# Layer 3 of a four-layer graph attention kernel: denominators from the exponentials' own sums, and head sums on half-width column tiles

## The chip, the cores and the metric

The kernel runs on one NeuronCore of a Trainium2 chip. TensorE multiplies matrices into PSUM, which has eight banks of 128 rows by 512 f32 values. VectorE and ScalarE compute on SBUF and PSUM. GpSimd does small steps on SBUF. SyncE issues the transfers. Each engine takes its instructions in the order in which the program lists them, and semaphores tie the engines to each other. The metric is the device time of one execution in microseconds. The profiled execution took 3,227.98 us; the three timed runs took 3,219.42, 3,227.3 and 3,229.8 us.

## The reference

There are 128 graphs of 128 nodes with 512 features, and four attention layers, one after the other; each normalizes the features, takes their positive part, attends over the neighbours, and adds the result to the features. The change is in the last layer, which has H = 8 heads of k = 64 features:

```python
def _L3_gnn_ref(x, A, W_proj, W_att, b_att):
    xp = jnp.einsum('bnd,do->bno', x, W_proj)
    xh = xp.reshape(B, N, H, k).transpose(0, 2, 1, 3)
    a_src = jnp.einsum('bhnk,hk->bhn', xh, W_att[:, :k])
    a_dst = jnp.einsum('bhnk,hk->bhn', xh, W_att[:, k:])
    scores = a_src[:, :, :, None] + a_dst[:, :, None, :] + b_att[None, :, None, None]
    scores = jax.nn.leaky_relu(scores, negative_slope=NEG_SLOPE)
    scores = jnp.where((A > 0)[:, None, :, :], scores, NEG_INF)
    att = jax.nn.softmax(scores, axis=-1)
    out = jax.nn.relu(jnp.einsum('bhij,bhjk->bhik', att, xh))
    return out.transpose(0, 2, 1, 3).reshape(B, N, H * k)

h = jnp.maximum(_layernorm(x, axis=-1), 0.0)
x = x + _L3_gnn_ref(h, adj, L3_gnn_W_proj, L3_gnn_W_att, L3_gnn_b_att)
```

The softmax is a division of two sums. For each node i and head, the numerator is the sum over j of exp(score) times the features of j, and the denominator is the sum over j of exp(score).

## The kernel before

One graph is one stream of steps: `graph` (line 1053) runs `layer0` to `layer3` for it, and the nodes lie on the 128 partitions. Up to 13 graphs (`FLYING`) are in flight at once. A planner written in the kernel (`Scheduler`, line 158) merges their streams into one order for each engine. It keeps a model of time: `Step.estimate` (line 70) gives each step a duration by engine, operation and size, and `issue` (line 288) takes, among the steps that could start first, the one of the graph that is most behind its due times. This order is fixed when the program is built. All steps are issued from one line, so every instruction of the profile has line 310, and groups are told apart by the names of their tiles.

Buffers come from pools with a fixed number of copies. The ones that matter here are `bank` (eight PSUM banks), `x3` (three buffers for layer 3's features, called `fx` in the code), `e3` (three for its attention matrices, eight heads of 128 x 128), `f3` (four small ones) and `t` (five). `give_back` returns a buffer when the last reader has been listed.

`layer3` (line 909) goes like this for a graph. The normalized features are transposed and projected; the 528 columns of the product are, for each head, two attention terms and 64 features. Two copies on ScalarE bring them into `fx`, where each head has 67 columns: two terms, 64 features, and a last one that GpSimd sets to one (line 917). The scores of all heads are built by VectorE with the mask and the row maxima. ScalarE then makes eight passes with Prelu and eight with Exp over the heads, each with a bias of its own for every row. The exponentials are turned round: they go through DRAM in blocks (`exchanged`, on SyncE's queue) and are transposed in squares by VectorE; the last five graphs (`late`) use TensorE's transpose instead.

The sums follow in two halves of four heads. For each half there is one bank and a group of four matmuls: stationary are the 128 x 128 turned exponentials of a head, moving are its 64 features and the column of ones. So the 65th column of each result is the denominator. VectorE inverts the four denominators out of the bank and multiplies the 4 x 64 sums with them into `t`. At the end one VectorE step adds the positive part to the node features `xt`, which SyncE writes out.

In the profile `fx` is named x, the exponentials are e (or ht for the late graphs, which are turned into that buffer), the small tile with terms, maxima and reciprocals is f. Layers 0 to 2 take their denominators in another way, in `attention` (line 683): Exp has an `accum_out`, which leaves the sum of the row beside the result. In the profile such an exponential is followed by an instruction of its own on ScalarE, ACTIVATION_READ_ACCUMULATOR. An f32 matmul appears as two pairs of LDWEIGHTS (PEld) and MATMUL (PE).

Of the kernel before, what the change touches and what calls it, by code (L numbers as in the profile page):

```python
# [11 lines left out]
AF = mybir.ActivationFunctionType  # L12
ALU = mybir.AluOpType
# [6 lines left out]
SLOPE = 0.2  # L20
# [22 lines left out]
def size(ap):  # L43
    n = 1
    for count in ap.shape[1:]:
        n *= count
    return n


class Step:  # L50
# [19 lines left out]
    def estimate(self, name, outs, ins, kw):  # L70

        if name == "dma_start":
            moved = size(outs[0]) * outs[0].shape[0] * 4
            if self.engine == "POOL":
                self.moves = moved / 165e3
                return 1.0, 3
            run = 4 * min(a.shape[-1] for a in outs + ins)
            self.moves = moved / (280e3 if run > 512 else 220e3 if run > 128 else 130e3)
            busy = 0.5 if max(len(a.shape) for a in outs + ins) > 2 else 0.35
            return busy, (2.2 if moved > 16384 else 1.3)  # L80
        n = max(size(a) for a in outs[:1] + ins)
        if self.engine == "PE":
            if name == "transpose":
                return 0.109, 0.2
            return 2 * max(0.00084 * size(outs[0]), 0.108), 0.2
        if self.engine == "DVE":
            if name == "bn_stats":
                return 0.6, 0.12
            if name == "bn_aggr":
                return 0.09, 0.12  # L90
            per = 1 / 960
            if name == "tensor_scalar" and n >= 256:
                per /= 2
            return n * per + 0.07, 0.12
        if self.engine == "ACT":
            pointers = sum(isinstance(kw.get(k), bass.AP) for k in ("bias", "scale"))
            busy = n * 0.00081 + 0.105 + (0, 0.075, 0.135)[pointers]
            return busy + 0.1 * ("accum_out" in kw), 0.15
        if self.engine == "POOL":
            if kw.get("op") == ALU.pow or ALU.pow in kw.get("ops", ()):  # L100
                return 0.6, 0.1
            return (0.25 if n <= 16 else 0.55 if name == "tensor_scalar" else 1.3), 0.1
        raise ValueError(name)
# [54 lines left out]
class Scheduler:  # L158
# [14 lines left out]
    def give_back(self, *aps):  # L173
        for ap in aps:
            name = ap.tensor.name
            tag = self.tag_of.pop(name)
            heapq.heappush(self.returned[tag], self.last_use.get(name, 0.0))
# [157 lines left out]
def kernel(  # L335
# [24 lines left out]
    B, P, D = x.shape  # L360
# [4 lines left out]
    H3 = l3_watt.shape[0]  # L365
    K3 = l3_watt.shape[1] // 2
# [12 lines left out]
    T = Engine("PE", nc.tensor)  # L379
    V = Engine("DVE", nc.vector)  # L380
    A = Engine("ACT", nc.scalar)
    G = Engine("POOL", nc.gpsimd)
    S = Engine("SP", nc.sync)
    sched = Scheduler()
    give_back = sched.give_back

    def bank():
        return Take(ps, [P, 512], "bank", 8)

    def tile_of(tag, bufs, *shape):  # L390
        return Take(work, [P, *shape], tag, bufs)
# [15 lines left out]
    E1, E2, E3 = 2 * H1, 2, 2  # L407
# [180 lines left out]
    def blocks_of(t):  # L588

        return [t[:, i : i + P] for i in range(0, t.shape[1], P)]  # L590

    def transposed(blocks, tag, bufs):

        n = len(blocks)
        r = yield tile_of(tag, bufs, n * P)
        pt = yield bank()
        yield Group(
            [T.transpose(pt[:, j * P : (j + 1) * P], b, ident) for j, b in enumerate(blocks)]
        )
        yield A.copy(r, pt[:, : n * P])  # L600
        give_back(pt)
        return blocks_of(r)
# [63 lines left out]
    def repeated(cols):  # L666
        n = cols.shape[1]
        return cols.unsqueeze(1).to_broadcast([P, Q // n, n])
# [240 lines left out]
    def layer3(xt, mask, late):  # L909

        h = yield from norm_relu(xt)
        ht = yield from transposed(blocks_of(h), "ht", 3)
        give_back(h)
        yield Until("wp")

        fx = yield tile_of("x3", 3, H3, E3 + K3 + 1)
        yield G.memset(fx[:, :, E3 + K3 :], 1.0)
        half = H3 // 2
        yield from projected(
            ht,  # L920
            KC,
            [w.rearrange("p h k -> p (h k)") for w in wpx],
            2,
            [fx[:, g : g + half, : E3 + K3] for g in (0, half)],
        )
        give_back(ht[0])
        f = yield tile_of("f3", 4, 4, H3)
        f, mx, rz = f[:, :2], f[:, 2], f[:, 3]
        yield G.tensor_tensor(f, fx[:, :, :E3].rearrange("p h s -> p s h"), b_l3, ALU.add)

        e = yield tile_of("e3", 3, H3 * P)
        if late:
            heads = e.rearrange("p (h c b) -> p h c b", h=H3, b=Q)
        else:
            heads = e.rearrange("p (c h b) -> p h c b", h=H3, b=Q)
            rows = yield from rows_in_dram(repeated(f[:, 0]), H3)
            yield S.dma_start(out=e.rearrange("p (c f) -> p c f", c=R), in_=rows)
        mask3 = mask.rearrange("p (c b) -> p c b", b=Q)

        for g in range(0, H3, 4):  # L940
            part = [heads[:, g + j] for j in range(4)]
            if late:
                pt = yield from spread(f[:, 0, g : g + 4])
                part = pt.rearrange("p (h c b) -> p h c b", h=4, b=Q)
                part = [part[:, j] for j in range(4)]
            yield Group(
                [
                    V.tensor_tensor_reduce(
                        out=heads[:, g + j],
                        in0=part[j],  # L950
                        in1=mask3,
                        scale=1.0,
                        scalar=LOWEST,
                        op0=ALU.add,
                        op1=ALU.max,
                        accum_out=mx[:, g + j : g + j + 1],
                    )
                    for j in range(4)
                ]
            )  # L960
            if late:
                give_back(pt)
        give_back(mask)
        yield G.tensor_tensor(mx, mx, f[:, 1], ALU.add)
        yield A.activation(out=mx, in_=mx, func=AF.Prelu, alpha=SLOPE)
        yield G.tensor_scalar(mx, mx, -1.0, None, ALU.mult)
        for bias, func in ((f[:, 1], dict(func=AF.Prelu, alpha=SLOPE)), (mx, dict(func=AF.Exp))):
            for k in range(H3):
                yield A.activation(
                    out=heads[:, k], in_=heads[:, k], bias=bias[:, k : k + 1], **func  # L970
                )
        et = []
        if late:
            for g in range(0, H3, 4):
                et += yield from transposed(blocks_of(e)[g : g + 4], "ht", 3)
        else:
            to = yield from exchanged(e, "et3", 2)

            yield V.transpose(
                e.rearrange("p (h r b) -> p r h b", h=H3, b=Q),  # L980
                to.rearrange("p (r h b) -> p r h b", h=H3, b=Q),
            )
            give_back(to)
            et = blocks_of(e)
        t = yield tile_of("t", 5, D)
        for i in range(2):
            pa = yield bank()
            p3 = pa[:, : half * (K3 + 1)].rearrange("p (h k) -> p h k", h=half)
            yield Group(
                [  # L990
                    T.matmul(
                        p3[:, k - i * half, :],
                        lhsT=et[k],
                        rhs=fx[:, k, E3:],
                        start=True,
                        stop=True,
                    )
                    for k in range(i * half, (i + 1) * half)
                ]
            )  # L1000
            r = rz[:, i * half : (i + 1) * half]
            yield V.reciprocal(r, p3[:, :, K3])
            yield V.tensor_tensor(
                t[:, i * half * K3 : (i + 1) * half * K3].rearrange("p (h k) -> p h k", k=K3),
                p3[:, :, :K3],
                r.unsqueeze(2).to_broadcast([P, half, K3]),
                ALU.mult,
            )
            give_back(pa)
        give_back(e, fx, f)  # L1010
        if late:
            give_back(et[0], et[4])
        yield V.scalar_tensor_tensor(xt, t, 0.0, xt, ALU.max, ALU.add)
        give_back(t)
# [133 lines left out]
```

## Time and profile before

| what | value |
|---|---|
| profiled execution | 3,227.98 us |
| its span, first to last instruction | 3,226.2 us |
| median of the timed runs | 3,227.3 us |
| TensorE multiplications, busy | 3,189.4 us, 15,386 instructions |
| TensorE weight loads, busy | 2,497.0 us |
| VectorE busy | 2,857.0 us |
| ScalarE busy | 2,468.5 us |
| GpSimd busy | 855.9 us |
| mean granted TensorE clock | 0.994 of full speed |
| layer 3's sums: multiplications (x,e and x,ht) | 2,048 of 65 columns |
| ScalarE's accumulator reads, layers 0 to 2 | 896, mean 187 ns |

Busy time of TensorE's multiplications is the union of their records. A record lasts longer than the distance to the next one, since multiplications overlap in the array; the distance between starts tells what one costs in a row of them. LDWEIGHTS have a row of their own because they run beside multiplications.

### The profile page before, as it was taken

How to read it: one execution, taken by the hardware profiler on the slowest of the kernel's cores; microseconds unless marked ns; L12 is line 12 of the kernel's file. 1: busy time of each engine (PE TensorE's matmuls, PEld its weight loads, DVE VectorE, ACT ScalarE, POOL GpSimd, SP SyncE). 2: the span in 40 equal slices, each digit the busy share in tenths (PEclk: the TensorE clock that was granted, in tenths of full speed). 3: DMA queues.
4: the chain of work that ended last, by engine and by line, in shares of the span. 5: the costliest groups of instructions: out<-in, count | busy, mean ns of one | idle time of the engine just before them, and what ended most of it. 6: DMA issues, size and time to landing. Idle time of an engine off the chain costs nothing.

```text
span 3226.2 us, 60294 instructions
## 1 busy us (share of the span) xinstructions
PE 3189.4 (99%) x15386; PEld 2497.0 (77%) x15386; DVE 2857.0 (89%) x11663; ACT 2468.5 (77%) x7224; POOL 855.9 (27%) x2313
## 2 busy tenths in 40 slices
PE   8999999999999999999999999999999999999998
PEld 6777777777777777777777777777777777777786
DVE  6888888999998989999998999998999989989876
ACT  5677777778777877777877777777777777778867
POOL 1232222222222222222222222222222222222222
PEclk8999999999999999999999999999999999999999
DMA  6245555556556656655555555555555655555432
GB/s 173 52 114 137 144 143 152 153 150 154 150 144 157 153 141 155 155 144 155 155 146 141 157 153 151 153 152 141 151 151 151 154 150 149 143 159 149 110 101 66
DMA packets 770082, 460.39 MB, mean 143 GB/s; under 512 B 344776, under 2 KB 702408, under 8 KB 769736
## 3 DMA queue, kind: packets, MB, share of 16 engines
q1 hardware_dynamic: 765560, 456.53, 54.6%
q8 instruction: 123, 2.02, 0.3%
q14 instruction: 223, 1.83, 0.2%
q10 hardware_dynamic: 4176, 0.02, 0.1%
HBM read 299.00 MB, written 157.33 MB: 141 GB/s over the span
## 4 chain that ended last, share of the span: by engine, by line
PE 91%; DVE 3%; DMA 3%; ACT 1%; issue 1%; POOL 0%; SPq 0%; ACTq 0%; DVEq 0%; POOLq 0%
PE bank L310 91%; DVE e L310 1%; DMA e<-d 1%; DMA d<-r 1%; DMA row<-d 1%; DMA et<-exchanged 0%; DVE st L310 0%; POOL st L310 0%; SPq L310 0%; DVE products L310 0%; DVE xt L310 0%; ACT e L310 0%; DVE t L310 0%; DVE y L310 0%; ACT ht L310 0%
## 5 line engine op out<-in xcount | busy, mean ns | idle before, releaser
L310 PE MATMUL bank<-w2x,y 128*128 128x257 f32 x4096 | 968.6, 381 | 1.7 <-DVE y L310 1.7
L310 PE MATMUL bank<-w1x,ht 128*128 128x344 f32 x3072 | 953.9, 454 | 2.6 <-ACT ht L310 2.6
L310 PEld LDWEIGHTS bank<-w2x,y 128*128 128x128 f32 x4096 | 763.9, 190 | 157.3 <-issue 32.8
L310 PEld LDWEIGHTS bank<-w1x,ht 128*128 128x128 f32 x3072 | 570.3, 191 | 257.2 <-issue 9.3
L310 ACT ACTIVATE e<-e,f 128x128 f32<-128x128 f32 x2176 | 707.2, 390 | 3.1 <-DVE c L310 3.1
L310 POOL TENSOR_SCALAR st<-st 128x1 f32<-128x1 f32 x1024 | 311.1, 308 | 1185.8 <-DVE st L310 993.9
L310 ACT ACTIVATE e<-e,c 128x128 f32<-128x128 f32 x1408 | 533.1, 394 | 116.9 <-DVE c L310 60.2
L310 PE MATMUL bank<-wpx,ht 128*128 128x264 f32 x2048 | 497.1, 386 | 0.3 <-ACT ht L310 0.3
L310 ACT ACTIVATE h<-xt,st 128x512 f32<-128x512 f32 x512 | 411.3, 810 | 83.9 <-POOL st L310 74.4
L310 PEld LDWEIGHTS bank<-wpx,ht 128*128 128x128 f32 x2048 | 387.8, 190 | 97.9 <-issue 22.2
L310 DVE CUSTOM_DVE_ANT_0 e<-e,m 128x128 f32<-128x128 f32 x1484 | 337.8, 286 | 23.5 <-DMA e<-d 23.3
L310 DVE BATCH_NORM_STATS2 st<-xt 128x6 f32<-128x512 f32 x512 | 340.8, 679 | 0.5 <-DMA xt<-in_x_dram 0.5
L310 POOL TENSOR_TENSOR st<-st,minus_half 128x1 f32<-128x1 f32 x512 | 297.0, 599 | 23.6 <-POOL st L310 0.2
L310 PEld LDWEIGHTS bank<-x,e 128*128 128x128 f32 x1968 | 254.8, 191 | 62.2 <-issue 29.8
L310 PEld LDWEIGHTS bank<-et,xl 128*128 128x128 f32 x2048 | 264.7, 192 | 36.5 <-issue 8.8
L310 PE MATMUL bank<-et,xl 128*128 128x128 f32 x2048 | 270.1, 275 | 0.4 <-ACT et L310 0.4
L310 PE MATMUL bank<-h,et 128*128 128x512 f32 x512 | 263.8, 598 | 3.3 <-ACT et L310 1.9
L310 PE MATMUL bank<-x,e 128*128 128x65 f32 x1968 | 246.8, 268 | 8.5 <-DVE e L310 2.1
L310 ACT COPY xl<-bank 128x344 f32<-128x344 f32 x384 | 167.7, 437 | 108.1 <-PE bank L310 103.9
L310 ACT COPY ht<-bank 128x512 f32<-128x512 f32 x274 | 159.6, 582 | 114.9 <-PE bank L310 113.7
L310 ACT ACTIVATE t<-t 128x512 f32<-128x512 f32 x256 | 160.3, 627 | 88.1 <-DVE t L310 87.3
L310 DVE TENSOR_TENSOR y<-bank,b 128x512 f32<-128x512 f32 x256 | 175.1, 684 | 36.0 <-PE bank L310 34.7
(85 smaller groups left out, 4342.4 us busy)
## 6 DMA issues: line engine op xcount, KB each, us to landing
e<-d SPq DMA_DIRECT2D x123, 512.0 KB
exchanged<-e SPq DMA_DIRECT2D x492, 128.0 KB
et<-exchanged SPq DMA_DIRECT2D x123, 512.0 KB
xt<-in_x_dram SPq DMA_DIRECT2D x128, 256.0 KB
out_dram<-xt SPq DMA_DIRECT2D x128, 256.0 KB
e<-d SPq DMA_DIRECT2D x125, 256.0 KB
exchanged<-e SPq DMA_DIRECT2D x480, 64.0 KB
et<-exchanged SPq DMA_DIRECT2D x120, 256.0 KB
```

Source lines behind the costliest of these rows:

```text
L310: method(*args, **kw)
```

## The change

Four things change, all for layer 3 and in the planner's model of it:

- The features `fx` lose the column of ones and the memset that sets it: 66 columns for each head.
- The exponentials get `accum_out=rz[:, k]`, so that ScalarE leaves the denominators in `rz`. One reciprocal of all eight follows the last exponential on VectorE.
- The sums of all heads go into one bank, 8 x 64 = 512 columns. Each head's matmul is split into two by the output rows: one with columns 0 to 63 of the turned exponentials as stationary operand, one with columns 64 to 127. The first writes rows 0 to 63 of the bank, the second rows 64 to 127. In the built program these have a tile size of 128 x 64 and the tile positions (0, 0) and (0, 64). All sixteen are one group, so nothing comes between them on TensorE.
- VectorE multiplies the whole bank with the eight reciprocals in one step.

The planner is told 0.07 us for a matmul with fewer than 128 output rows; before, it was told 0.216 us for a matmul of up to 128 columns.

```diff
@@ Step.estimate @@
             if name == "transpose":
                 return 0.109, 0.2
+            if outs[0].shape[0] < 128:
+                return 0.07, 0.2
             return 2 * max(0.00084 * size(outs[0]), 0.108), 0.2
@@ layer3 @@
-        fx = yield tile_of("x3", 3, H3, E3 + K3 + 1)
-        yield G.memset(fx[:, :, E3 + K3 :], 1.0)
+        fx = yield tile_of("x3", 3, H3, E3 + K3)
...
-            [fx[:, g : g + half, : E3 + K3] for g in (0, half)],
+            [fx[:, g : g + half] for g in (0, half)],
...
-        for bias, func in ((f[:, 1], dict(func=AF.Prelu, alpha=SLOPE)), (mx, dict(func=AF.Exp))):
-            for k in range(H3):
-                yield A.activation(
-                    out=heads[:, k], in_=heads[:, k], bias=bias[:, k : k + 1], **func
-                )
+        for k in range(H3):
+            yield A.activation(
+                out=heads[:, k],
+                in_=heads[:, k],
+                func=AF.Prelu,
+                bias=f[:, 1, k : k + 1],
+                alpha=SLOPE,
+            )
+        for k in range(H3):
+            yield A.activation(
+                out=heads[:, k],
+                in_=heads[:, k],
+                func=AF.Exp,
+                bias=mx[:, k : k + 1],
+                accum_out=rz[:, k : k + 1],
+            )
+        yield V.reciprocal(rz, rz)
...
-        for i in range(2):
-            pa = yield bank()
-            p3 = pa[:, : half * (K3 + 1)].rearrange("p (h k) -> p h k", h=half)
-            yield Group(
-                [
-                    T.matmul(
-                        p3[:, k - i * half, :],
-                        lhsT=et[k],
-                        rhs=fx[:, k, E3:],
-                        start=True,
-                        stop=True,
-                    )
-                    for k in range(i * half, (i + 1) * half)
-                ]
-            )
-            r = rz[:, i * half : (i + 1) * half]
-            yield V.reciprocal(r, p3[:, :, K3])
-            yield V.tensor_tensor(
-                t[:, i * half * K3 : (i + 1) * half * K3].rearrange("p (h k) -> p h k", k=K3),
-                p3[:, :, :K3],
-                r.unsqueeze(2).to_broadcast([P, half, K3]),
-                ALU.mult,
-            )
-            give_back(pa)
+        pa = yield bank()
+        p3 = pa.rearrange("p (h k) -> p h k", h=H3)
+        yield Group(
+            [
+                T.matmul(
+                    p3[lo : lo + P // 2, k, :],
+                    lhsT=et[k][:, lo : lo + P // 2],
+                    rhs=fx[:, k, E3:],
+                    start=True,
+                    stop=True,
+                )
+                for k in range(H3)
+                for lo in (0, P // 2)
+            ]
+        )
+        yield V.tensor_tensor(
+            t.rearrange("p (h k) -> p h k", h=H3),
+            p3,
+            rz.unsqueeze(2).to_broadcast([P, H3, K3]),
+            ALU.mult,
+        )
+        give_back(pa)
```

## The prediction

> **What bounds the kernel.** I began with the page: busy time per engine, and the slices of the span.
>
> ```profile
> span 3226.2 us, 60294 instructions
> PE 3189.4 (99%) x15386; PEld 2497.0 (77%) x15386; DVE 2857.0 (89%) x11663; ACT 2468.5 (77%) x7224; POOL 855.9 (27%) x2313
> ...
> PE   8999999999999999999999999999999999999998
> ```
>
> TensorE's multiply queue is busy for 99% of the span, in every slice but the first and the last. Busy shares overstate a pipelined engine, so the chain of waits comes next; its columns are start, length, engine and count.
>
> ```profile
> 525.63 2633.99 PE bank L310 x12782
> ```
>
> From 525.63 us on, 2,634 us of the chain are TensorE work in its own order, with no wait in between. Before it and behind it the chain hops over other engines, but the multiplier's idle time in all is only 31.6 us (the sum of its waits). How much room do the others have? The busy time by stretch says:
>
> ```profile
> core 0: us, PE busy (x) PEld busy (x) DVE busy (x) ACT busy (x) POOL busy (x), PEclk, DMA share, GB/s
> ...
> 1000.00:2000.00 1000.00, 1000.00 (x4837) 785.56 (x4836) 910.04 (x3742) 784.52 (x2297) 272.85 (x738) 1.00 0.58 151
> ```
>
> In this stretch TensorE never stops, VectorE has 9% free, ScalarE 22%. So time on TensorE's path counts in full, and the others' time only once one of them runs out of room. What a pass of the layer-3 sums costs is read from TensorE's timeline (start, length, name, count); spacing of starts, not length, is the price, since passes overlap.
>
> ```profile
> 1601.64 1.00 PE L310 MATMUL bank<-x,e 128*128 128x65 f32 x8
> 1602.48 1.95 PE L310 MATMUL bank<-w2x,y 128*128 128x257 f32 x8
> 1604.27 2.48 PE L310 MATMUL bank<-w1x,ht 128*128 128x344 f32 x8
> ...
> 1607.86 1.02 PE L310 MATMUL bank<-h,et 128*128 128x512 f32 x2
> 1608.72 1.05 PE L310 MATMUL bank<-et,xl 128*128 128x128 f32 x8
> 1609.61 2.48 PE L310 MATMUL bank<-w1x,ht 128*128 128x344 f32 x8
> ```
>
> An f32 matmul is two passes, each a weight load and a multiplication. Eight passes with 65 moving columns take 1602.48 - 1601.64 = 0.84 us, or 0.105 each. Eight with 128 columns (et,xl) take 1609.61 - 1608.72 = 0.89 us, 0.111 each. Half the columns are no cheaper, so something else than the columns sets both: the load of 128 stationary columns. The pure price of a moving column comes from the 512-column passes: (1608.72 - 1607.86) / 2 / 512 = 0.84 ns. A 65-column pass would need 0.055 us if its load were free; the load makes it 0.105.
>
> **The change, part by part.** The other prices are in the groups by form (busy us, mean ns, idle before).
>
> ```profile
> L310 PE MATMUL bank<-w2x,y 128*128 128x257 f32 x4096 | 968.6, 381 | 1.7 <-DVE y L310 1.7
> ...
> L310 PEld LDWEIGHTS bank<-x,e 128*128 128x128 f32 x1968 | 254.8, 191 | 62.2 <-issue 29.8 <-POOL f L310 4.0 <-POOL st L310 3.3
> ...
> L310 ACT ACTIVATION_READ_ACCUMULATOR e<-e,c 128x1 f32 x896 | 168.0, 187 | 0.0
> ...
> L310 DVE TENSOR_TENSOR t<-bank,f 128x256 f32<-128x256 f32 x256 | 105.1, 411 | 5.7
> ...
> L310 DVE RECIPROCAL f<-bank 128x4 f32<-128x4 f32 x256 | 44.2, 173 | 33.4 <-PE bank L310 30.7
> ...
> L310 DVE RECIPROCAL c<-c 128x4 f32<-128x4 f32 x128 | 21.2, 165 | 2.2 <-ACT e L310 1.2
> ...
> L310 DVE TENSOR_TENSOR y<-bank,b 128x512 f32<-128x512 f32 x256 | 175.1, 684 | 36.0 <-PE bank L310 34.7
> ...
> L310 POOL MEMSET x<- 128x8 f32 x128 | 14.4, 113 | 186.6 <-PE bank L310 186.6
> ```
>
> *TensorE, what goes.* Each graph has 8 heads x 2 passes x 0.105 = 1.68 us of such sums; 128 graphs make 215 us.
>
> *TensorE, what comes.* Each head becomes two matmuls, one for each half of the output rows: 8 x 2 x 2 = 32 passes, each loading 64 columns and streaming 64. Streaming 64 columns costs 64 x 0.84 = 0.054 us. Loading 64 costs 0.105 / 2 = 0.053 us if a load's price goes by its columns. No record of before uses half of the array, so the pass is bounded: 0.027 us if the two halves load and stream side by side (two passes in 0.054), 0.054 if they take turns, 0.105 if a half load costs as much as a whole one. The 32 passes are then 0.86, 1.73 or 3.36 us. I take 0.86: the nearest rows show loads running beside multiplications already (weight loads 2,497 us and multiplications 3,189 us in a span of 3,226 us), the two halves write different rows, and neighbours in the order always use different halves.
>
> *Going into the halves and out again.* No row shows what it costs. The lower bound is nothing: in the timeline above, passes of different shapes follow each other at their usual spacing. The upper bound is an array that empties at each end: a 257-column pass lasts 0.381 us but is spaced 0.224 (1604.27 - 1602.48 over 8), a tail of 0.16, and the next load, 0.19, is no longer hidden; 0.35 an end, 0.70 a graph. I take the tail alone at both ends, 0.32, since loads ran beside multiplications in every row.
>
> So a graph's sums take 0.86 + 0.32 = 1.18 us in place of 1.68: 0.50 us, times 128 = 64 us off the path. (The planner's new 0.07 us for a half orders the steps; no price is taken from it.)
>
> The Trainium skill bears on both choices, once each way. "TensorEngine Tiling (Array Packing)", Key Properties, says that tiles load and multiply independently, and that a change of tiling mode drains the engine; with the drain at my upper price the saving is 1.68 - 0.86 - 0.70 = 0.12 us a graph, 15 us in all. "TensorE: Matmul & The Clock Gate", Part 3, says that a load overlaps a running multiplication only where its row group differs; the halves of this change share all 128 rows, so by it load and stream would add up, 16 x 0.107 + 0.32 = 2.03 us, 45 us slower. The overlapping loads of before use all rows too, so the trace already contradicts that page for whole-width loads; no run so far shows it for halves.
>
> *ScalarE.* The 1,024 exponentials of layer 3 get a running sum, which adds a read of the accumulator: 1,024 x 0.187 = 191 us, and 4 ns on each exponential (394 against 390). In the 1,000 us stretch 41 graphs pass, so ScalarE goes from 785 to 785 + 41 x 8 x 0.191 = 847 us of about 980, 86%. Hidden behind TensorE; without that cover it would be 1.5 us a graph.
>
> *VectorE.* Two reciprocals (0.173) and two products of 256 columns (0.411) become one reciprocal of 8 (0.165, the row of 4) and one product of 512 out of a bank (0.684, the y<-bank,b row): 1.168 - 0.849 = 0.32 us less, 41 us in all. It goes to 897 of 980 us, 92%. Worth nothing on the path.
>
> *GpSimd.* 128 memsets of 0.113 us go, with their 186.6 us of waiting for the features' buffer at the head of that queue, in front of the norms' small steps. The copy that fills the buffer, on ScalarE, takes over the wait; it stood behind the memset already, so it starts no later. Off the path: nothing.
>
> *New waits.* The reciprocal now waits for the eighth exponential instead of for a bank; behind it stand VectorE's steps of other graphs, the product comes much later. On SyncE the exchange of the exponentials starts 8 x 0.191 = 1.5 us later, with other graphs' transfers queued behind. The planner allows 0.1 us for a read that takes 0.187, so both queues may stand 8 x 0.087 = 0.7 us longer than planned. Cover: thirteen graphs in flight and a TensorE queue with no gap. If the cover went, 0.7 x 128 = 90 us. No DMA is added. One bank is held instead of two in turn.
>
> *The tail.* In the last graph ScalarE's chain is bare: +1.5 us, less 0.3 on VectorE: +1 us.
>
> Sum: the profiled execution took 3,228.0 us (span 3,226.2), close to the median of 3,227.3. 3,228 - 64 + 1 = **3,165 us**. Its bounds: 1.68 - 0.86 = 0.82 us a graph gives 3,123; 0.12 gives 3,213.
>
> **The rivals.**
> *The halves take turns* (slower). One multiplication or one load at a time, whatever half it is for: 1.73 + 0.32 = 2.05 us a graph, +0.37 x 128 = +47, 3,275 us; with an array that empties fully 3,324, with free switches 3,234. It decides as soon as a pass costs (1.68 - 0.32) / 32 = 0.0425 us or more. For it: TensorE is one queue in order, and no row of before shows two multiplications side by side. Against it: the halves share no output row, and loads do run beside multiplications.
> *A half load costs a whole one* (far slower): 3.36 + 0.32 is 2.0 us more a graph, about 3,484 us. For it: the 65-column pass shows a cost that ignores the moving width. Against it: nothing direct.
> *The gain is lost to lateness.* The denominators are late by 0.7 us a graph, VectorE at 92% cannot catch up, and TensorE gets gaps: between half and all of the 64 us goes, 3,195 to 3,228 us. For it: VectorE already waits 76 us for exponentials in other layers' reciprocals. Against it: it has 9% free, and TensorE waited 31.6 us in all.
>
> **How the numbers follow.** Forecast 0.58, turns 0.27, lateness 0.10, whole loads 0.05. The likeliest time is 3,165 us, its own range 3,123 to 3,213. About 0.3% (10 us, the spread of the three runs) can be told from no change. Faster: 0.58 + half of lateness = 0.63; same: the other half and a sliver of turns, 0.07; slower 0.30. For 8 in 10 the range reaches from 3,125 into the cheaper part of turns, 3,290.
>
> **What would show it.** Right: starts in the layer-3 run average 0.03 us, the run with what precedes and follows takes near 1.2 us, and TensorE still has no gap. Wrong: starts 0.05 us or more apart (turns), near 0.1 (whole loads), a long first pass or a late next one (the switch), or gaps on TensorE that end on the exponentials or the reciprocals (lateness).

## The result, and the profile after

The changed kernel is slower. Its median is 3,266.5 us against 3,228.6 us for the kernel before on the same chip, a ratio of 1.0127 with a 95% interval of 1.0104 to 1.0150. That is 38 us more, where 63 us less had been forecast. The profiled execution took 3,266.5 us.

The page of the changed kernel: span, busy time, and the chain of waits by engine.

```profile
span 3264.6 us, 64927 instructions
PE 3155.1 (97%) x17434; PEld 2394.0 (73%) x17434; DVE 2839.4 (87%) x11407; ACT 2542.8 (78%) x8248; POOL 894.9 (27%) x2185
...
PE 43%; DMA 24%; DVE 19%; ACT 8%; issue 3%; SPq 2%; POOL 2%; DVEq 0%; ACTq 0%; POOLq 0%
```

The same chain before:

```profile
PE 91%; DVE 3%; DMA 3%; ACT 1%; issue 1%; POOL 0%; SPq 0%; ACTq 0%; DVEq 0%; POOLq 0%
```

TensorE's busy time fell by 34 us, while the span grew by 38; the rest of the span, in which TensorE stands, grew from 37 to 110 us. The chain, which was 91% TensorE before, is now 43% TensorE; transfers, VectorE and ScalarE have the rest. This share shows that TensorE now waits for others, but it does not measure the loss: of the kernels below, e3 is the fastest with 60%, and e4 is 4.9% slower than the kernel before with 75%.

The stretch from 1,000 to 2,000 us, with the columns named:

```profile
core 0: us, PE busy (x) PEld busy (x) DVE busy (x) ACT busy (x) POOL busy (x), PEclk, DMA share, GB/s
...
1000.00:2000.00 1000.00, 972.43 (x5396) 738.09 (x5395) 889.51 (x3594) 793.69 (x2588) 285.10 (x686) 1.00 0.57 148
```

TensorE, which had no gap here before, stands for 27.6 us of 1,000. VectorE (890) and ScalarE (794) have as much room as before. So no engine is full, and yet the work goes slower: in the traces, layer 3 of one graph follows that of another after 24.40 us before and 24.75 us now (the mean over graphs 30 to 110).

TensorE's waits in the changed kernel (waited for, us in total, times, longest):

```profile
PE bank L312 <- DMA et<-dealt: 39.8, 27, 3.3
PE bank L312 <- ACT ht L312: 31.4, 34, 2.6
PE bank L312 <- ACT h L312: 5.8, 6, 1.4
```

They end on dealt exponentials of layers 0 and 2 and on copies of turned features (ht). These steps have nothing to do with layer 3's sums. Now the sums themselves, on TensorE's timeline (start, length, name, count; the last line is the queue of weight loads):

```profile
1608.44 2.48 PE L312 MATMUL bank<-w1x,ht 128*128 128x344 f32 x8
1610.75 1.02 PE L312 MATMUL bank<-x,et 128*128 128x512 f32 x2
1611.62 0.60 PE L312 MATMUL bank<-ident,h 128*128 128x128 f32 x4
...
1615.52 2.48 PE L312 MATMUL bank<-w1x,ht 128*128 128x344 f32 x8
1617.92 1.15 PE L312 MATMUL bank<-x,e 128*64 128x64 f32 x32
1619.01 1.12 PE L312 MATMUL bank<-h,et 128*128 128x512 f32 x2
1619.97 0.60 PE L312 MATMUL bank<-ident,h 128*128 128x128 f32 x4
...
1617.92 1.01 PEld L312 LDWEIGHTS bank<-x,e 128*64 128x64 f32 x32 [0.48 <-issue]
```

A run of 32 half-width passes takes 1619.01 - 1617.92 = 1.09 us. Getting in costs the w1x group ahead of it 1617.92 - 1615.52 = 2.40 us instead of 1610.75 - 1608.44 = 2.31; getting out makes the two h,et passes last 1619.97 - 1619.01 = 0.96 instead of 0.87. In all 1.28 us; the median over 115 such runs is 1.279 (0.093 in, 1.082, 0.104 out). Two whole groups took 2 x 0.847 = 1.69 us before, by the same measure: 0.41 us a graph more.

That comparison is not quite fair to the halves, because what stands behind a group differs between the two orders. A whole group of before costs 0.85 us ahead of the short ident,h group, where most of them stand, but 0.89 ahead of w2x,y. Experiment e9 below has whole matmuls at exactly the places where the changed kernel has halves. The same place in it:

```profile
1629.88 2.48 PE L312 MATMUL bank<-w1x,ht 128*128 128x344 f32 x8
1632.20 1.89 PE L312 MATMUL bank<-x,e 128*128 128x64 f32 x16
1633.93 1.08 PE L312 MATMUL bank<-h,et 128*128 128x512 f32 x2
1634.84 0.60 PE L312 MATMUL bank<-ident,h 128*128 128x128 f32 x4
```

Here the run takes 1633.93 - 1632.20 = 1.73 us, getting in costs nothing, and the two h,et passes behind it last 0.91. By the same measure the median over 117 runs is 1.79 us (0.00 in, 1.73, 0.06 out). So in the changed kernel's own order the halves save 0.51 us a graph, 65 us in all. The part of the change that the forecast rested on did what was expected, and still the kernel lost.

The other new prices, from the groups by form (busy us, mean ns, idle before):

```profile
L312 ACT ACTIVATION_READ_ACCUMULATOR e<-e,f 128x1 f32 x1024 | 193.3, 189 | 0.0
...
L312 DVE TENSOR_TENSOR t<-bank,f 128x512 f32<-128x512 f32 x128 | 86.7, 677 | 22.4 <-PE bank L312 22.3
...
L312 DVE RECIPROCAL f<-f 128x8 f32<-128x8 f32 x128 | 24.7, 193 | 8.2 <-ACT e L312 8.2
```

VectorE stands for only 8.2 us, in all 128 graphs together, before it can invert the eight denominators. The exponentials' sums are not what is late.

### The profile page after: what moved, and what is told of

It reads as the page before. It is cut to its first block, busy times and chain, and to the rows that moved or that the text cites. A ratio compares the mean times of both kernels' runs of the same rounds, so it can differ in the third digit from the quotient of the medians.

```text
span 3264.6 us, 64927 instructions
## 1 busy us (share of the span) xinstructions
PE 3155.1 (97%) x17434; PEld 2394.0 (73%) x17434; DVE 2839.4 (87%) x11407; ACT 2542.8 (78%) x8248; POOL 894.9 (27%) x2185
## 2 busy tenths in 40 slices
DMA packets 770103, 460.69 MB, mean 141 GB/s; under 512 B 344776, under 2 KB 702408, under 8 KB 769736
## 4 chain that ended last, share of the span: by engine, by line
PE 43%; DMA 24%; DVE 19%; ACT 8%; issue 3%; SPq 2%; POOL 2%; DVEq 0%; ACTq 0%; POOLq 0%
PE bank L312 43%; DMA d<-r 8%; DVE e L312 6%; DMA row<-d 5%; ACT e L312 5%; DMA e<-d 5%; DMA et<-dealt 5%; DVE st L312 2%; DVE xt L312 2%; DVE products L312 2%; SPq L312 2%; DVE t L312 2%; DVE y L312 1%; POOL st L312 1%; DVE c L312 1%
## 5 line engine op out<-in xcount | busy, mean ns | idle before, releaser
L312 PE MATMUL bank<-w2x,y 128*128 128x257 f32 x4096 | 956.1, 382 | 5.0 <-DVE y L312 4.9
L312 ACT ACTIVATE e<-e,f 128x128 f32<-128x128 f32 x2176 | 772.7, 391 | 3.9 <-DVE c L312 3.9
L312 ACT ACTIVATE e<-e,c 128x128 f32<-128x128 f32 x1408 | 539.7, 395 | 157.1 <-DVE c L312 81.4
L312 POOL TENSOR_SCALAR st<-st 128x1 f32<-128x1 f32 x1024 | 331.6, 329 | 1096.6 <-DVE st L312 907.6
L312 DVE BATCH_NORM_STATS2 st<-xt 128x6 f32<-128x512 f32 x512 | 347.4, 679 | 1.2 <-DMA xt<-in_x_dram 1.2
L312 POOL TENSOR_TENSOR st<-st,minus_half 128x1 f32<-128x1 f32 x512 | 307.9, 607 | 28.0
L312 PE MATMUL bank<-h,et 128*128 128x512 f32 x512 | 270.9, 612 | 39.7 <-DMA et<-dealt 36.6
L312 DVE CUSTOM_DVE_ANT_1 e<-row,m 128x128 f32<-128x128 f32 x361 | 138.9, 390 | 97.3 <-DMA row<-d 97.0
L312 DVE SCALAR_TENSOR_TENSOR xt<-bank,c,xt 128x512 f32<-128x512 f32 x256 | 185.5, 733 | 35.9 <-PE bank L312 35.8
L312 PEld LDWEIGHTS bank<-ident,h 128*128 128x128 f32 x1024 | 126.8, 141 | 113.0 <-issue 69.0
```

The costliest lines, as they stand in the source:

```text
L312: method(*args, **kw)
```

## The experiments

The ratios are to the kernel before on the same chip, with 95% intervals. "Order" is the order in which each engine's queue lists its instructions.

| kernel | order planned with | ratio | interval |
|---|---|---|---|
| changed kernel | half matmul at 0.070 us | 1.0127 | 1.0104 to 1.0150 |
| e1 sums alone | whole, 0.216 | 1.0054 | 1.0039 to 1.0069 |
| e2 tiles alone | half, 0.070 | 1.0290 | 1.0273 to 1.0308 |
| e3 changed | half, 0.108 | 0.9949 | 0.9935 to 0.9964 |
| e4 changed | half, 0.070; transfers 1.5 us slower | 1.0487 | 1.0471 to 1.0502 |
| e5 changed | half, 0.080 | 1.0173 | 1.0149 to 1.0197 |
| e6 changed | half, 0.125 | 1.0135 | 1.0120 to 1.0150 |
| e7 before | whole, 0.140 | 1.0352 | 1.0331 to 1.0373 |
| e8 changed, 14 graphs | half, 0.070 | 1.0100 | 1.0081 to 1.0119 |
| e9 whole matmuls | exactly the changed kernel's | 1.0238 | 1.0220 to 1.0256 |
| e10 whole matmuls | exactly e3's | 1.0084 | 1.0069 to 1.0099 |
| e11 before with halves | exactly that of before | 0.9963 | 0.9950 to 0.9976 |
| e12 before | whole, 0.220 | 1.0551 | 1.0536 to 1.0567 |
| e13 cheap turned load | exactly the changed kernel's | 1.0147 | 1.0132 to 1.0162 |
| e14 cheap turned load | exactly e12's | 1.0532 | 1.0514 to 1.0549 |
| e15 cheap turned load | exactly that of before | 1.0003 | 0.9994 to 1.0012 |
| e16 changed | half, 0.106 | 1.0115 | 1.0099 to 1.0132 |
| e17 one product later | the changed kernel's but for TensorE | 1.0185 | 1.0167 to 1.0204 |
| e18 one product later | e12's but for TensorE | 1.0657 | 1.0636 to 1.0678 |

### The parts by themselves: e1 and e2

e1 takes the denominators from the exponentials and keeps whole matmuls of 64 columns in two banks.

```diff
-        fx = yield tile_of("x3", 3, H3, E3 + K3 + 1)
-        yield G.memset(fx[:, :, E3 + K3 :], 1.0)
+        fx = yield tile_of("x3", 3, H3, E3 + K3)
...
+                bias=mx[:, k : k + 1],
+                accum_out=rz[:, k : k + 1],
...
+        yield V.reciprocal(rz, rz)
...
-            yield V.reciprocal(r, p3[:, :, K3])
```

> The kernel before, with the denominators taken from the exponentials' own sums and without the column of ones; the matmuls stay whole (128 output rows, now 64 columns), in two groups and two banks. Theory (TensorE's saving was real, and TensorE lost its lead over the other engines, so that it now stands waiting for late transfers and copies): TensorE is as loaded as before, so nothing shows; 3,215 to 3,240 us, TensorE without gaps from 1,000 to 3,000 us. Rival (the running sums make ScalarE, the reciprocal and the exchange late): slower, 3,250 us or more, with gaps on TensorE.

It took 3,241.4 us, just above what the theory allowed, and TensorE was busy for 999 of 1,000 us. Up to graph 120 it is level with the kernel before (the sums of that graph start at 3,157 us in both traces); the loss, 13 us between the two spans, lies in the last graphs. There few graphs are left to cover ScalarE's longer chain, but the order differs there too, and the two were not told apart.

e2 keeps the column of ones and both banks, and splits the matmuls.

```diff
-                        p3[:, k - i * half, :],
-                        lhsT=et[k],
+                        p3[lo : lo + P // 2, k - i * half, :],
+                        lhsT=et[k][:, lo : lo + P // 2],
...
+                    for lo in (0, P // 2)
```

> The kernel before, with its column of ones, its two banks and its two reciprocals out of the banks; only the matmuls are split into half-width tiles of 65 columns, and the planner is told 0.07 us for each. Theory (lost lead): gaps on TensorE as in the changed kernel, 3,230 to 3,290 us. Rival (running sums are what is late): the saving shows, 3,150 to 3,185 us, with no gaps.

It took 3,316.0 us, slower than either theory allowed. Getting in and out is paid twice here. Compared at like places, a group of 16 half passes takes 0.77 us ahead of ident,h and 0.81 ahead of w2x,y, where a whole group of before took 0.85 and 0.89. So the halves save 0.08 us a group, 0.16 a graph, 20 us in all. That explains why it gained little, not why it lost 3%. TensorE has gaps (969 busy of 1,000 us) as in the changed kernel.

### The planner's price: e3 to e8

Five kernels change what the planner believes, and e8 changes the number of graphs in flight, with the buffers that are sized by it; no instruction of the work changes. The first edit is that of e3; e5 has 0.08 and e6 has 0.125 in its place. The second is e4's, the third e8's, all in the changed kernel. The last is e7's, in the kernel before.

```diff
-                return 0.07, 0.2
+                return 0.108, 0.2
...
-            return busy, (2.2 if moved > 16384 else 1.3)
+            return busy, (3.7 if moved > 16384 else 2.8)
...
-FLYING = 13
+FLYING = 14
...
+            if size(outs[0]) == 65:
+                return 0.14, 0.2
```

> The changed kernel, with the planner told 0.108 us for a half matmul, so that a graph's sums cost 1.73 us in its model, as before. The instructions are the same, only their order is that of a planner that believes TensorE to be as loaded as before. Theory (the order planned with cheap tiles asks for more than the other queues deliver): part of the loss goes, 3,190 to 3,245 us. Rival (running sums): nothing changes, 3,255 to 3,275 us.

> The changed kernel, with the planner told 1.5 us more for the landing of every transfer (3.7 and 2.8 us in place of 2.2 and 1.3). The chain of waits of the changed kernel has dealt exponentials that land after 5.5 to 7 us once in every four graphs. Theory in the form that the planner's too short transfers let TensorE run into them: the gaps behind et<-dealt get smaller, 3,160 to 3,240 us. Rival (running sums): 3,255 us or more. If neither, the order decides for reasons that neither theory names.

> The changed kernel with the planner told 0.080 us for a half matmul: the changed kernel's trace shows 1.28 us for a run of 16 (0.093 to get in, 1.082 from the first start to the next group's, 0.104 to get out), and 1.28 / 16 = 0.080. Theory that the price told was too low: a good part of the way from 3,266 to 3,209 us, 3,200 to 3,240. Rival (which order comes out is chance, and only the loss of TensorE's lead makes chance count): anything from 3,190 to 3,290, with no regard to the price.

> The changed kernel with the planner told 0.125 us for a half matmul (2.00 us a graph, more than before). Theory (an order planned with a dearer TensorE gives the other queues room): as with 0.108 or better, 3,180 to 3,215 us. Rival (chance): anywhere from 3,190 to 3,290.

> The kernel before, instruction by instruction, but with its 65-column matmuls told as 0.14 us each, 1.12 us a graph, which is what the changed kernel tells for its own. Theory (a cheap-TensorE order is harmless as long as TensorE itself is the one slow engine, since the real matmuls then hold everything up and the others catch up): 3,220 to 3,245 us, TensorE without gaps. Rival (this kind of order is bad by itself, with or without tiles): 3,255 us or more, with gaps on TensorE.

> The changed kernel with 14 graphs in flight instead of 13 and everything else the same. Theory (TensorE runs into late results because too little finished work lies ahead of it): more graphs put more work ahead, 3,190 to 3,245 us. Rival (the number in flight does not matter, the order of the queues does): within 3,250 to 3,290, or no better than chance.

e3 gave 3,209.0 us, faster than the kernel before; the same instructions in the changed kernel's order are 1.8% slower. It looked as if a dearer TensorE in the plan were the remedy, and e5 and e6 contradict that: the price that the trace shows (0.080) gives 1.0173, a still dearer one (0.125) gives 1.0135. Telling the planner of slower transfers gave the worst of these, 1.0487. A fourteenth graph in flight changed little. The theory of a lost lead then fell with e7. That is the kernel before without a single half-width matmul, in an order planned with a cheap TensorE; its matmuls are as dear as ever, so by the theory TensorE had to stay the one slow engine. The same stretch of its trace (columns as above):

```profile
1000.00:2000.00 1000.00, 969.65 (x4626) 754.68 (x4625) 875.26 (x3579) 752.66 (x2199) 258.80 (x705) 0.99 0.58 144
```

TensorE stands for 30 us of 1,000 in it, and the kernel loses 3.5%. What e3 has in the same stretch:

```profile
1000.00:2000.00 1000.00, 990.75 (x5529) 757.49 (x5528) 911.42 (x3683) 816.58 (x2647) 270.35 (x704) 1.00 0.58 151
```

### The order held still: e9, e10, e11

To see what the halves are worth by themselves, three kernels keep an order row by row in every queue and differ in nothing but whole or half matmuls. The planner gets the same price for the group, so it lists the same. The edit is that of e9, in the changed kernel; e10 has 0.216 in place of 0.14. e11 is e2 with 0.108 in place of 0.07.

```diff
-            if outs[0].shape[0] < 128:
-                return 0.07, 0.2
+            if size(outs[0]) == 64:
+                return 0.14, 0.2
...
-                    p3[lo : lo + P // 2, k, :],
-                    lhsT=et[k][:, lo : lo + P // 2],
+                    p3[:, k, :],
+                    lhsT=et[k],
```

> The changed kernel's order of every queue, row by row, with one thing other: a head's sums are one matmul of 128 output rows again instead of two halves (one bank, running sums as in the changed kernel; the planner is told 0.14 us for one, so the run costs 1.12 us in its model, as the changed kernel's did). This shows what the halves are worth where the order stays. By the spacing of starts in the traces a whole run costs 2 x 0.847 = 1.69 us and the halves 1.28. Theory (the halves save about 0.41 us a graph, and the order took more than that away): 3,285 to 3,325 us, slower than the changed kernel by 20 to 55 us. Rival (the halves save nothing in the whole, since in this order TensorE is not what is late): 3,255 to 3,280 us.

> The same with the order of the kernel whose half matmuls were told as 0.108 us (whole ones told as 0.216), again identical row by row but for whole matmuls. Theory: 3,235 to 3,265 us, slower than that kernel's ratio of 0.995 by 0.8 to 1.6%. Rival (halves worth nothing): a ratio of 0.99 to 1.00 to the kernel before.

> The kernel before with its order of every queue kept, and its two groups of four whole matmuls turned into two groups of eight halves with 65 columns (told as 0.108 us, so that nothing moves). In the run with two such groups, a group costs 0.81 us against 0.85 whole, because getting in and out is paid twice. Theory (in the order of before TensorE sets the pace, and what it saves is seen): 0.03 x 2 x 128 = 9 us faster, a ratio of 0.995 to 0.999. Rival (halves are slower for what stands around them): 1.00 or more.

All three came out as the theory had it. In the changed kernel's order whole matmuls cost 1.0238 against 1.0127: the halves are worth 1.1%, 36 us. In e3's order it is 1.0084 against 0.9949: 1.35%, 44 us. In the order of before, with getting in and out paid twice, 0.4%, 12 us. (The 9 us in e11's text set groups with different followers against each other; by like places it is the 20 us above.)

The spacings ask for 65, 65 and 20 us, so between half and two thirds of the saving reaches the time. Where the rest goes, the busy times of the profiled executions show. From e9 to the changed kernel TensorE's busy time falls by 66 us (3,220.8 to 3,155.1), and the rest of the span, in which it stands, grows from 80 to 110 us. From e10 to e3 it falls by 62 us (3,205.1 to 3,142.8), and the rest grows from 52 to 64. From the kernel before to e11 it falls by 17.5 us, and the rest grows from 37 to 51. So even with the order held still a part of what TensorE saves turns into waits.

e9 and e10 have the same instructions and differ by 1.5%; the changed kernel and e3 have the same instructions and differ by 1.8%. These two pairs show what the order alone is worth. With whole matmuls the changed kernel's order and running sums are 2.4% slower than the kernel before; the halves win back less than half of that.

### How much an order can do: e12 and e16

e12 is the kernel before, instruction by instruction, with one price nudged by 2%.

```diff
+            if size(outs[0]) == 65:
+                return 0.22, 0.2
```

> The kernel before, instruction by instruction, with its 65-column matmuls told as 0.220 us instead of 0.216 (0.03 us a graph in the planner's model). Nothing but the order can change. Theory (the order of before is a good one out of many, and a small nudge gives another): slower, 3,240 to 3,350 us. Rival (only orders with a much cheaper TensorE are bad): 3,215 to 3,240 us.

It took 3,410.7 us, 5.5% more. Its timeline on TensorE, about 1,030 us:

```profile
1028.97 2.48 PE L312 MATMUL bank<-w1x,ht 128*128 128x344 f32 x8
1035.68 2.08 PE L312 MATMUL bank<-et,xl 128*128 128x128 f32 x8 [4.24 <-DMA et<-exchanged]
1037.55 1.81 PE L312 MATMUL bank<-x,e 128*128 128x65 f32 x8
1039.16 1.06 PE L312 MATMUL bank<-ident,h 128*128 128x128 f32 x4
```

TensorE stands for 4.24 us until the exchanged exponentials of layer 1 have landed. Then eight passes with 65 columns take 1039.16 - 1037.55 = 1.61 us instead of 0.84. The row of the stretch behind the gap says why:

```profile
core 0: us, PE busy (x) PEld busy (x) DVE busy (x) ACT busy (x) POOL busy (x), PEclk, DMA share, GB/s
...
1036.00:1040.00 4.00, 4.00 (x20) 4.00 (x20) 2.18 (x12) 0.50 (x2) 0.57 (x3) 0.50 0.50 136
```

The granted clock is 0.50 there. Such a gap came about once in 104 us, that is, once in four graphs, 102.7 us in 27 waits in all. The page of e12 shows what the slow stretches add:

```profile
PE 3264.0 (96%) x15386; PEld 2550.5 (75%) x15386; DVE 2868.7 (84%) x11663; ACT 2476.9 (73%) x7224; POOL 853.5 (25%) x2313
```

The same multiplications are busy for 74.6 us longer than in the kernel before (3,189.4). The mean granted clock is 0.973 against 0.994, which over 3,407 us is about as much (72 us, an estimate from these two figures). The span grew by 181.2 us (3,226.2 to 3,407.4), and the other 106.6 us are more standing.

e16 goes back to the changed kernel with a price next to e3's.

```diff
-                return 0.07, 0.2
+                return 0.106, 0.2
```

> The changed kernel with the planner told 0.106 us for a half matmul, next to the 0.108 that gave a ratio of 0.995. Theory (order by chance): anywhere from 0.99 to 1.03, with no likeness to its neighbour. Rival (orders planned at TensorE's old load are the good ones): 0.985 to 1.000.

0.106 gives 1.0115 where 0.108 gives 0.9949. There is no likeness between neighbours. In the prices tried no rule is seen for which order comes out, and the spread is wide: 0.995 to 1.049 of the kernel before with the changed kernel's instructions, 1.000 to 1.055 with those of the kernel before.

### What such an order loses to: e13 to e15, e17 and e18

The chain of waits of the changed kernel between two stays on TensorE, with a few of its 58 pieces (start, length, what):

```profile
1042.45 2.43 DMA d<-r
...
1044.89 5.84 DMA e<-d
...
1052.50 0.66 DVE xt L312
...
1056.71 0.60 DVE t L312
...
1057.80 5.98 DMA et<-dealt
...
1063.83 2.31 PE bank L312 x11
```

The chain goes from a small transfer over a load of score rows of 5.84 us, VectorE's queue with other graphs' steps in it (most pieces from 1,051 to 1,057 us are of that kind) and SyncE to a transfer of 5.98 us, and only then back to TensorE. It repeats with a period of some 98 us, four graphs. Once in four graphs the adjacency is loaded turned, in runs of 128 bytes, and this load was the first suspect. Three kernels make it cheap in an order that stays.

```diff
+        for m, step in enumerate(steps):
+            step.calls = S.dma_start(
+                out=t[m * Q : (m + 1) * Q],
+                in_=adj[b : b + AG, m * Q : (m + 1) * Q].rearrange("g i j -> i g j"),
+            ).calls
```

> The changed kernel's order of every queue, row by row; the load of the turned adjacency, once in four graphs, reads the same 256 KB in runs of 512 bytes instead of 128 and without the turning of blocks. The masks of layer 1 are then other than the reference's (part of the computation is changed). Theory (that load, with 16,384 packets' worth of small runs and a long stand of SyncE's queue, is what makes the dealt exponentials late once in four graphs): the gaps go and TensorE's saving appears, 3,170 to 3,215 us. Rival (the order makes the exponentials late whatever the load): 3,250 to 3,270 us.

> The same in the order of the kernel before nudged by 2% in one price (ratio 1.055, a gap of 4.2 us on TensorE at et<-exchanged once in four graphs, just behind that load on SyncE's queue). The masks of layer 1 are other than the reference's. Theory (the turned load is the cause): a ratio of 0.99 to 1.02. Rival (the order itself): 1.04 or more.

> The same in the order of the kernel before. The masks of layer 1 are other than the reference's. TensorE has no gaps there, so both theories expect no change: a ratio of 0.995 to 1.003. It shows what the cheaper load is worth by itself.

(256 KB in runs of 128 bytes are 2,048 runs; the 16,384 in that text is a slip.) The load did become cheaper: the execution moves the same bytes in 720,951 packets instead of 770,103 (e13 against the changed kernel). The times stayed: 1.0147 for 1.0127, 1.0532 for 1.0551, and 1.0003. The price of the turned load is not the cause. (e15 also shows how little the share of the chain tells: in it TensorE has 78% instead of 91%, in the same time.)

The second suspect was the place itself: TensorE reaches a product too early. Two kernels list it one group later on TensorE and leave every other queue as it is.

```diff
+        if step.engine == "PE" and not self.held and any(
+            r.startswith(HOLD) for r in step.reads
+        ):
+            self.held, self.passed = step, 0
+        else:
             for method, args, kw in step.calls:
                 method(*args, **kw)
+            if self.held and step.engine == "PE":
+                self.passed += 1
+                if self.passed == PAST:
+                    self.release()
```

Here HOLD names the turned exponentials (et0 in e17, et1 in e18) and PAST is 1; a held step is also released ahead of any step that needs what it writes, and ahead of a reuse of its buffers.

> The changed kernel with the order of all queues but TensorE's kept. On TensorE, a product with dealt exponentials (h,et or x,et) is listed behind the next group where no other step and no buffer needs it first; this moves it once in four graphs, at the place of the gap, behind an et,xl group of 0.89 us, and a few times elsewhere. In the changed kernel that place has gaps of 0.5 to 1.4 us and up to 3.3, 39.8 us in all. Theory (an order loses at the few places where TensorE reaches a step before its data): most of these gaps are filled, 20 to 40 us less than the changed kernel, a ratio of 1.000 to 1.007. Rival (something slower than TensorE goes round through all the queues, and the gap only moves on): 1.010 to 1.016, the same gap elsewhere.

> The kernel before nudged by 2% in one price (ratio 1.055), with the order of all queues but TensorE's kept; there a product with the exchanged exponentials of layer 1 steps behind the next group where it can. At the gap of 4.2 us, once in four graphs, 0.84 us of layer 3's sums come first. Theory: the gap shrinks by 0.84 us of some 104, a little more with what of the half clock behind the gap goes: a ratio of 1.040 to 1.050. Rival (a loop through all the queues): 1.053 or more.

Both became slower, by 0.6% (1.0185 / 1.0127) and 1.0% (1.0657 / 1.0551): the opposite of what the theory asked for. TensorE's waits in e17, then in e18:

```profile
PE bank L331 <- ACT ht L331: 36.5, 42, 2.7
PE bank L221 <- DMA et<-dealt: 30.7, 23, 4.1
...
PE bank L221 <- DMA et<-exchanged: 93.1, 42, 4.2
PE bank L331 <- DMA et<-dealt: 29.4, 30, 3.1
```

In e17 the waits for dealt exponentials fell from 39.8 to 30.7 us, in e18 those for exchanged ones from 102.7 to 93.1, but others took their place, and the whole got longer. Of 98 us 0.6% is 0.6 us, of 104 us 1.0% is 1.0 us; the product was put off by 0.89 and 0.84 us. A loss of this size in every round would fit a loop that runs through all the queues: what is late on TensorE makes its readers late, and those reach TensorE again one period later. The chain above, with TensorE in it for less than half, fits this too. But the loop is argued and not shown: which links close it was not found, nor what would open it.

## Why the prediction was wrong

The failed step is one parenthesis: "The planner's new 0.07 us for a half orders the steps; no price is taken from it." The order was put at nothing, without a reason. The runs show 1.5 to 1.8% for it alone: the changed kernel (1.0127) has the instructions of e3 (0.9949), and e9 (1.0238) those of e10 (1.0084). In the changed kernel's order the halves save 1.1% (e9), which is less than that. The same neglect stands in "Cover: thirteen graphs in flight and a TensorE queue with no gap": the gapless queue was a property of the order before, not of the load. e7 and e12 have the same load and have gaps. So the 64 us off TensorE's path did not all become time: TensorE stood for 37 us of the span before and for 110 after. Why the planned order leaves these gaps is open; the chain of waits runs through all the queues, and no run shows which link of it decides.

*The halves.* "I take 0.86" for the run and 0.32 for getting in and out, 1.18 us together; measured 1.28, that is, 16 pairs of 0.058 and 0.35 besides. What goes was mis-sized by as much: 1.68 was taken for the whole passes, and at the same places they take 1.79 (e9). So the forecast's 0.50 us a graph meets the 0.51 measured there by luck, since the two misses of 0.1 us cancel; against the groups of before at their own places it is 0.41. Side by side was right: the records start in pairs 7 ns apart, a pair every 58 ns, 0.029 us a pass against the 0.027 taken. The upper price of 0.70 for getting in and out is excluded. So the rival of taking turns, whose time (3,275 us) lies nearest to the result, is refuted: it asked for starts 0.05 us apart.

*Whole loads.* A half load that costs a whole one is refuted by the same pairs.

*Lateness.* The rival had the right kind of trouble, gaps on TensorE, for the wrong reason. It named late denominators; VectorE waited 8.2 us for these in all. The gaps end on other layers' exponentials and on turned features, and e2, e7 and e12 have such gaps without any running sums in layer 3.

*ScalarE.* The forecast added 191 us for the accumulator reads; the busy time grew by 74 (2,468.5 to 2,542.8). A read's record lasts 189 ns but lies beside its neighbours, as ScalarE's timeline in the changed kernel shows:

```profile
1609.74 0.39 ACT L312 ACTIVATE e<-e,f 128x128 f32<-128x128 f32 x1
1610.03 0.19 ACT L312 ACTIVATION_READ_ACCUMULATOR e<-e,f 128x1 f32 x1
1610.12 0.39 ACT L312 ACTIVATE e<-e,f 128x128 f32<-128x128 f32 x1
```

Exponentials with a read start 0.38 us apart; without one, passes of this size start 0.29 us apart in both traces. A read therefore costs 0.09 us in the row and not 0.187, less than the 0.1 us that the planner allows. The 0.7 us a graph by which queues were to stand longer than planned rested on that 0.187 and did not come.

*VectorE.* 41 us less was forecast, 18 came (2,857.0 to 2,839.4), with the new steps near their prices: 0.677 for 0.684 and 0.193 for 0.165. It did not matter, as said.

*The tail.* +1 us was forecast for the running sums; e1 loses 13 us in the last graphs, in an order of its own.

*The range.* 3,266 lies within 3,125 to 3,290 by luck: the range reached that far only for the rival of taking turns, which is refuted, and a lost order had no share in it.

The version that beats both kernels is e3, the changed kernel planned at 0.108: a ratio of 0.9949. e11 has 0.9963, with an interval that overlaps. That e3's order is a good one was found by trying, and a price of 0.106 in place of 0.108 loses it (e16).

## What to carry to other kernels

Where a planner fixes the order of several queues in advance, a change has two effects: what the instructions cost, and which order the planner now writes. The second can be larger, and it does not follow the first in size or in sign; measure the change with the order held still (same prices to the planner, other instructions), and then look for a good order separately, among several nudged prices. An engine that is busy for 99% of the time is only the bound of the order in which it was seen.

## What the runs showed of the hardware

- f32 passes on halves of 128 rows by 64 columns load and multiply side by side: a pair of passes every 58 ns. A run of 16 pairs costs 0.35 us besides (1.28 - 16 x 0.058): 0.093 ahead, 0.152 for the last pass instead of 0.029 or 0.058, 0.104 behind, and some 0.05 at the second pair. Of what stands behind, a run of whole passes pays 0.056 too (e9). The Trainium skill, "TensorE: Matmul & The Clock Gate", Part 3 (What overlaps and what doesn't), has loads beside multiplications only where the row group differs; here all passes use all rows, and they overlap. "TensorEngine Tiling (Array Packing)", Key Properties, has a drain at a change of mode without a figure; this cost at both ends agrees with it, though no run shows that it is a drain.
- After 4.24 us without work the granted clock of TensorE was 0.50 for the next stretch, and the passes there took 1.61 us instead of 0.84. In e12 a gap therefore costs more than its length: 107 us more of standing came with 75 us more of busy time for the same multiplications.
- ACTIVATION_READ_ACCUMULATOR has a record of 187 to 189 ns, but exponentials with one start only 0.09 us further apart than passes without; 1,024 more of them added 74 us of busy time on ScalarE, 72 ns each.
